# Turning x and h by VectorE blocks and a DRAM exchange instead of TensorE in a batched GRU and graph-convolution kernel

## The chip, the cores and the metric

The kernel runs on one core of a Trainium2 chip. The metric is the device time in microseconds of one execution of the whole program; lower is better. TensorE multiplies matrices into PSUM, VectorE and ScalarE do elementwise work, GpSimd (POOL) casts and issues DMAs, and SyncE (SP) only issues DMAs. Each engine works through its own queue in order.

## The reference

There are 16 graphs ("batches") of N = 1024 nodes with C = 128 features in fp32, each with a 1024 x 1024 adjacency matrix of zeros and ones. Two stages follow each other:

```python
h = relu(layernorm(x))
for i in range(4):                       # GRU stage
    hw = h @ weight[i]
    m = adj^T @ hw                       # einsum("bjn,bjd->bnd")
    gx, gh = m @ w_ih[i].T + b_ih[i], h @ w_hh[i].T + b_hh[i]
    r, z = sigmoid(xr + hr), sigmoid(xz + hz)
    n = tanh(xn + r * hn)
    h = (1 - z) * n + z * h
x = x + h * mask

h = relu(layernorm(x))
for i in range(4):                       # convolution stage
    h = relu(adj @ (h @ W[i]) + b[i])
    h = gamma * (h - mean) / sqrt(var + eps) + beta    # mean and var over all batches and nodes
x = x + h
```

Layer norm and the residual sum work on one node's 128 features, so they want nodes on the partitions. The gates' products contract over features, so they want features on the partitions. Between the two layouts an array of 1024 x 128 has to be turned, once on the way in (relu of the norm of x, to h_in) and once on the way out (the last h, to be added to x).

## The kernel before

**Streams.** The GRU stage keeps two batches in flight, in two `Stream` objects: `sa` has the even batches, `sb` the odd ones. `half_step(one, two)` (L856) interleaves them: it splits stream one's h for the aggregation (`split_step`), runs the gates of stream two (`gate_step`, L781), aggregates for stream one (`agg_step`), and in between calls the pieces that look ahead. Eight half-steps take two batches through four layers, so there are eight such cycles, and the last has no next batches.

**One half-step on TensorE.** The gates are 12 products (six for each half of 512 nodes), each of two passes (L790). `split_step` turns h into nodes on the partitions (hw_g, L498, 8 transposes), and ScalarE and VectorE split it into a high part (fp32r) and a low remainder, both named ghw (L502, L503). At layer 0 there is no such turn, since the norm's output y already has nodes on the partitions. `agg_step` then makes 32 products of 128 x 128 by 128 x 512 into two banks, pm (L525): eight row blocks, high and low, two halves. ScalarE copies pm to m (L770), which the next gates of that stream read.

**The gates' elementwise part.** ScalarE: sigmoid to r (L802), tanh (L807), sigmoid to z (L808). VectorE: L803, L804, then h minus r, times z, plus r (L810 to L812).

**Looking ahead.** When the stream that gates is past its layer i, `ahead` runs: after layer 0 (i = 1) `load_x` issues the load of x of batch b + 2 on POOL; after layer 1 (i = 2) `prepare` computes its norm: VectorE's statistics (L609, L610), ScalarE's root (L613), VectorE's reciprocal and shift (L616, L621), and eight ScalarE blocks y_in (L625); after layer 2 (i = 3) `prepare_turn` turns y_in by TensorE (pt_in, L647) into h_in (ScalarE copy, L648).

**The adjacency.** `look_on` acts for the stream that aggregates. At its layer 1 it issues eight raw copies on POOL (`copy_rows`, DRAM to DRAM, adj of batch b + 2 into raw), then for each of the batch's eight rows a POOL cast to bf16 (L594) and a DMA transpose on SP (L595), and last, on POOL, the write of the turned adjacency adjT_d (L848). At other layers VectorE looks over the rows (L589), reducing the low 16 bits of every entry to a maximum that a flag is made from at the end. `load_rows` (L581, in `take`) brings the next batch's rows from raw, eight loads of 512 KB on SP. A row tile comes free after the last layer's aggregation has read it.

**A batch's end.** After layer 3 `finish` runs `tail_norm`: TensorE turns the last h (pt_x, L657, two halves of four transposes), VectorE multiplies by the mask and adds to x (L660), statistics follow, and POOL writes xmid_d (L673). One half-step later the function `rest` does the remaining norm to y_mid (root, reciprocal, eight ScalarE blocks) and POOL writes ymid_d (L677). xmid_d and ymid_d feed the second stage.

**What sets the order.** Past a hand-ordered start, the queues of POOL and SP are in the order of the program text (`manual_schedule`). The order on TensorE, VectorE and ScalarE is set when the program is built, by a scheduler that may pull instructions forward or back; `behind` ties a piece to come after a given instruction. On POOL one cycle's order is: xmid of the even batch, ymid of the even batch, xmid of the odd, ymid of the odd, both x loads, eight raw copies, eight casts and adjT_d for the even batch, the same for the odd batch.

**The second stage** aggregates with the turned adjacency, loaded as bf16 from adjT_d by SP: `load_adjT` puts odd batches into one large block tile and even batches into half tiles (packed), then casts to fp32r (L1026, L1028).

Of the kernel before, what the change touches and what calls it, by code (L numbers as in the profile page):

```python
# [8 lines left out]
F32 = mybir.dt.float32  # L9
# [5 lines left out]
ALU = mybir.AluOpType  # L15
AX = mybir.AxisListType
P = 128
# [324 lines left out]
def exact_path(  # L342
# [191 lines left out]
    with ExitStack() as st:  # L534
# [42 lines left out]
        def load_rows(b):  # L577
# [4 lines left out]
                ts.append(t)  # L582
            return ts

        def look(b, row, j, part=0):

            lows = row.bitcast(U16).rearrange("p (n t) -> p n t", t=2)[:, :, 0]
            k = (b + part * B) * NB + j
            nc.vector.tensor_reduce(low[:, k : k + 1], lows, axis=AX.X, op=ALU.max)  # L589
# [46 lines left out]
            norm_scale(nt, 0, NB)  # L636
            norm_blocks(xt, y, nt, range(NB))

        def turn(y, name, hT=None, func=AF.Copy):

            if hT is None:
                hT = work.tile([P, N], F32, tag="h", name=f"h_{name}", bufs=7)
            for hf in range(NH):
                pt = tmp(f"pt_{name}_{hf}")
                for q in range(BH):
                    k = hf * BH + q
                    nc.tensor.transpose(pt[:, q * P : (q + 1) * P], y[:, k * P : (k + 1) * P], ident)  # L647
                nc.scalar.activation(hT[:, hf * HALF : (hf + 1) * HALF], pt, func)  # L648
            return hT

        def tail_norm(b, xt, hT):

            for hf in range(NH):
                pt = tmp(f"pt_x{b}_{hf}")
                for q in range(BH):
                    k = hf * BH + q
                    nc.tensor.transpose(pt[:, q * P : (q + 1) * P], hT[:, k * P : (k + 1) * P], ident)  # L657
                for q in range(BH):
                    k = hf * BH + q
                    nc.vector.scalar_tensor_tensor(  # L660
                        xt[:, k, :],
                        pt[:, q * P : (q + 1) * P],
                        maskT[:, b * NB + k : b * NB + k + 1],
                        xt[:, k, :],
                        ALU.mult,
                        ALU.add,
                    )
            nt = norm_stats(xt, f"mid{b}")
            if b + 1 < B:
# [3 lines left out]
            nc.gpsimd.dma_start(xmid_d[b].rearrange("(k p) c -> p k c", p=P), xt)  # L673

            def rest():
                norm_apply(xt, y, nt)
                nc.gpsimd.dma_start(ymid_d[b], y)  # L677

            return rest
# [10 lines left out]
        class Stream:  # L690


            def __init__(self, first):
                self.b, self.i, self.rest, self.tag = first, 0, None, "AB"[first % 2]
                self.opened = None

            def open(self, xt):

# [28 lines left out]
            def prepare(self, b, xt):  # L727
                y = work.tile([P, N], F32, tag=f"y{self.tag}", name=f"y_in{b}", bufs=1)
                norm(xt, y, f"in{b}")
                self.ready = b, xt, y  # L730

            def prepare_turn(self):
                b, xt, y = self.ready
                self.ready = xt, y, turn(y, f"in{b}")

            def take(self):
                self.xt, self.y, self.hT = self.ready
                self.rows = load_rows(self.b)
                self.looks = 0

            def split_step(self):
                nm = f"{self.b}_{self.i}"
# [38 lines left out]
            def gate_step(self, hf, between=None):  # L781
                i, nm = self.i, f"{self.b}_{self.i}_{hf}"
                if hf == 0 and not self.opened:
                    self.new = work.tile([P, N], F32, tag="h", name=f"h{nm}", bufs=7)
                cols = slice(hf * HALF, (hf + 1) * HALF)
                hin, m = self.hT[:, cols], self.m[hf]
                pr, pz, phn, pxn = self.opened or (acc(t, f"{t}{nm}") for t in ("g_r", "g_z", "g_hn", "g_xn"))

                def part(po, wT, g, rhs, start, stop):
                    nc.tensor.matmul(po, wT[:, i, g * C : (g + 1) * C], rhs, start=start, stop=stop)  # L790
# [12 lines left out]
                nc.vector.scalar_tensor_tensor(r, phn, b_hn(i), r, ALU.add, ALU.mult)  # L803
                nc.vector.tensor_add(r, pxn, r)  # L804
                if between:
                    between()
                nc.scalar.activation(r, r, AF.Tanh, bias=b_in(i))  # L807
                self.last_act = nc.scalar.activation(z, pz, AF.Sigmoid, bias=brz[:, 3 * i + 1 : 3 * i + 2])  # L808
                ho = self.new[:, cols]
                nc.vector.tensor_sub(ho, hin, r)  # L810
                nc.vector.tensor_mul(ho, ho, z)
                self.last_dve = nc.vector.tensor_add(ho, ho, r)  # L812
                if hf == NH - 1:
                    self.hT = self.new
                    self.i += 1

            def ahead(self):

                if self.b + 2 >= B:
                    return  # L820
                if self.i == 1:
                    self.next_x = load_x(self.b + 2, nc.gpsimd)
                if self.i == 2:
                    with behind(self.last_act, self.last_dve):
                        self.prepare(self.b + 2, self.next_x)
                if self.i == 3:
                    self.prepare_turn()

            def finish(self):

                if self.i == L:
                    assert self.looks == NB
                    self.rest = tail_norm(self.b, self.xt, self.hT)
                    self.b, self.i = self.b + 2, 0
                    if self.b < B:
                        self.take()

            def look_on(self, two):

                if self.i == 0:  # L840
                    return
                if self.i == 1:
                    if self.b + 2 < B:
                        copy_rows(self.b + 2)
                    adjT = turned_tile(f"adjT{self.b}")
                    for j in range(NB):
                        transpose_rows(self.b, self.rows[j], j, adjT)
                    nc.gpsimd.dma_start(adjT_d[self.b], adjT)  # L848
                if two.i == 2 and two.b + 2 < B:
                    return  # L850
                with behind(two.last_dve):
                    for j in range(self.looks, min(self.looks + 4, NB)):
                        look(self.b, self.rows[j], j)
                        self.looks += 1

        def half_step(one, two, gated=None, halfway=None):  # L856
# [9 lines left out]
            one.agg_step(0)  # L866
            if halfway:
                halfway()
            if one.rest:
                with behind(two.last_act):  # L870
                    one.rest()
                one.rest = None
            two.ahead()
            one.look_on(two)
            one.agg_step(1)
# [119 lines left out]
        with tc.manual_schedule(engines={mybir.EngineType.Pool, mybir.EngineType.SP}):  # L995
# [4 lines left out]
            sb.gate_step(0)  # L1000
            sb.gate_step(1)
            with tc.issue_after(sb.last_act.ins):
                sa.rest()
            sb.finish()


# [134 lines left out]
    def fetch_x(b):  # L1141
# [6 lines left out]
                t = t.rearrange("p l c -> p (l c)")  # L1148
                hs.extend(t[:, k * HALF : (k + 1) * HALF] for k in range(3))
        elif b == B - 1:  # L1150
            hs = [half_tile(f"xo_h{k}").bitcast(F32) for k in range(8)]
            row = keep.tile([P, N], F32, tag="row", name="xo_row", bufs=12)
            wide = turned_tile("xo_wide").rearrange("p a n -> p (a n)").bitcast(F32)
            hs.extend(t[:, k * HALF : (k + 1) * HALF] for t, n in ((row, 2), (wide, 8)) for k in range(n))
        else:
            return
        xo.extend(hs[k : k + 2] for k in range(0, len(hs), 2))
# [10 lines left out]
    for b in range(B):  # L1168
# [4 lines left out]
        if waiting:  # L1173
            last = first_weights(*waiting, stats)
            if b == 1:
                with tc.issue_after(last.ins):
                    sb.rest()
        if b == B - 1:
            hw_next = raw_split(1)
        aggregate(pm, hw, rows, 1)  # L1180
# [115 lines left out]
```

## Time and profile before

| what | value |
|---|---|
| median of 3 runs | 1840.78 us (1840.69 to 1840.88) |
| the profiled execution's own time | 1840.61 us |
| its span, first to last instruction | 1838.8 us |
| GRU stage / convolution stage, about | 1210 us / 628 us |
| mean granted TensorE clock | 0.999 |
| TensorE busy in 308 to 458 us / in 1210 to 1838 us | 150.00 of 150.00 us / 616.50 of 628.00 us |
| VectorE, ScalarE, POOL busy in 308 to 458 us | 100.77, 75.00, 31.48 us |
| mean share of the DMA engines busy in 308 to 458 us | 0.60 |
| pt_in and pt_x transposes | 128 and 128, 272 ns each (median) |

The span is 1.8 us shorter than the profiled execution's time; what is added or taken within the span comes in full in the time. A timeline line has the start in us, the busy time in us, the engine, the line, the operation, the tiles written and read, the shape and a count; in brackets stands how long the engine was idle before it and what ended that. Transposes in a row are pipelined, so eight of them that last 272 ns each take 1.03 us together, and the time from one group's start to the next group's start is what a group costs TensorE. L525 and L790 are the lines of helpers that record every aggregation product and every gate product, so one reads them by the tile's name.

### The profile page before, as it was taken

How to read it: one execution, taken by the hardware profiler on the slowest of the kernel's cores; microseconds unless marked ns; L12 is line 12 of the kernel's file. 1: busy time of each engine (PE TensorE's matmuls, PEld its weight loads, DVE VectorE, ACT ScalarE, POOL GpSimd, SP SyncE). 2: the span in 40 equal slices, each digit the busy share in tenths (PEclk: the TensorE clock that was granted, in tenths of full speed). 3: DMA queues.
4: the chain of work that ended last, by engine and by line, in shares of the span. 5: the costliest groups of instructions: out<-in, count | busy, mean ns of one | idle time of the engine just before them, and what ended most of it. 6: DMA issues, size and time to landing. Idle time of an engine off the chain costs nothing.

```text
span 1838.8 us, 21960 instructions
## 1 busy us (share of the span) xinstructions
PE 1821.5 (99%) x7326; PEld 1254.2 (68%) x7326; DVE 1225.6 (67%) x2244; ACT 1035.8 (56%) x1577; POOL 285.0 (15%) x378
## 2 busy tenths in 40 slices
PE   9999999999999999999999999999999999999997
PEld 6566666656566666666565666667778888888886
DVE  7656667567666766766766757676666666666665
ACT  5544454553545554445355353467777767767764
POOL 4131320230231042023023013011100000000011
PEclk9999999999999999999999999999999999999999
DMA  7189775575486386567557546349876676767676
GB/s 264 39 247 317 209 229 195 162 206 192 159 233 180 126 233 178 196 172 217 218 159 206 178 145 172 103 159 332 291 248 228 212 256 204 257 209 260 210 249 242
DMA packets 256280, 381.21 MB, mean 207 GB/s; under 512 B 149932, under 2 KB 155856, under 8 KB 252320
## 3 DMA queue, kind: packets, MB, share of 16 engines
q1 hardware_dynamic: 237968, 245.95, 44.2%
q0 software_dynamic: 17664, 133.53, 20.4%
q8 instruction: 59, 0.97, 0.2%
q14 instruction: 61, 0.50, 0.1%
q10 hardware_dynamic: 528, 0.26, 0.0%
HBM read 287.39 MB, written 117.44 MB: 220 GB/s over the span
## 4 chain that ended last, share of the span: by engine, by line
PE 94%; DVE 2%; ACT 2%; issue 1%; DMA 1%; SPq 0%; POOL 0%; DVEq 0%; ACTq 0%; POOLq 0%
PE pm L525 24%; PE pc_m L525 12%; PE g_r L790 11%; PE g_z L790 11%; PE pc_g_r L525 6%; PE pc_g_z L525 6%; PE g_hn L790 6%; PE g_xn L790 6%; PE hw_c L500 4%; PE hw_g L498 2%; PE pw_g_hn L1096 1%; PE pw_g_xn L1096 1%; PE pt_in L647 1%; PE pt_x L657 1%; PE pc_g_r L510 1%
## 5 line engine op out<-in xcount | busy, mean ns | idle before, releaser
L525 PE MATMUL pm<-row,ghw 128*128 128x512 f32 x2048 | 515.6, 406 | 0.1
L525 PEld LDWEIGHTS pm<-row,ghw 128*128 128x128 f32 x2048 | 383.2, 188 | 112.6 <-issue 36.9
L525 PE MATMUL pc_m<-wide,chw 128*128 128x512 f32 x1024 | 246.0, 395 | 0.0
L525 PEld LDWEIGHTS pc_m<-wide,chw 128*128 128x128 f32 x1024 | 190.5, 188 | 42.3 <-issue 4.3
L807 ACT ACTIVATE r<-r,vecs 128x512 f32<-128x512 f32 x128 | 92.3, 721 | 216.8 <-DVE r L804 216.8
L525 PE MATMUL pc_g_r<-wide,chw 128*128 128x512 f32 x464 | 187.0, 403 | 0.3 <-ACT chw L502 0.3
L525 PE MATMUL pc_g_z<-wide,chw 128*128 128x512 f32 x464 | 180.9, 390 | 0.0
L594 POOL CAST half<-row 128x1024 bf16<-128x1024 f32 x128 | 139.7, 1108 | 250.9 <-DMA adjT<-half 169.6
L1028 DVE CAST wide<-packed 128x1024 fp32r<-128x1024 bf16 x160 | 110.0, 692 | 74.5 <-PE pc_m L525 56.4
L1028 DVE CAST wide<-block 128x1024 fp32r<-128x1024 bf16 x160 | 110.2, 691 | 73.2 <-PE pc_g_z L525 40.2
L503 DVE TENSOR_TENSOR ghw<-hw_g,ghw 128x512 fp32r<-128x512 f32 x96 | 62.0, 686 | 129.7 <-ACT ghw L502 129.5
L1026 ACT CAST wide<-block 128x1024 fp32r<-128x1024 bf16 x96 | 100.6, 1048 | 59.3 <-PE pc_m L525 34.3
L803 DVE SCALAR_TENSOR_TENSOR r<-g_hn,vecs,r 128x512 f32<-128x512 f32 x128 | 95.4, 745 | 56.8 <-ACT r L802 31.3
L1026 ACT CAST wide<-packed 128x1024 fp32r<-128x1024 bf16 x96 | 100.7, 1049 | 55.6 <-PE pc_g_z L525 23.7
L790 PE MATMUL g_r<-m,w_mT 128*128 128x512 f32 x256 | 130.7, 592 | 0.0
L790 PE MATMUL g_z<-m,w_mT 128*128 128x512 f32 x256 | 130.7, 592 | 0.0
L790 PE MATMUL g_xn<-m,w_mT 128*128 128x512 f32 x256 | 130.7, 592 | 0.0
L589 DVE TENSOR_REDUCE low<-row 128x1 f32<-128x1024 uint16 x112 | 128.6, 1210 | 0.0
L808 ACT ACTIVATE z<-g_z,brz 128x512 f32<-128x512 f32 x128 | 87.1, 680 | 71.0 <-PE g_z L790 71.0
L770 ACT COPY m<-pm 128x512 f32<-128x512 f32 x128 | 68.8, 586 | 101.3 <-PE pm L525 101.2
L802 ACT ACTIVATE r<-g_r,brz 128x512 f32<-128x512 f32 x128 | 87.7, 685 | 60.3 <-PE g_r L790 59.5
L810 DVE TENSOR_TENSOR h<-h,r 128x512 f32<-128x512 f32 x96 | 74.6, 777 | 62.4 <-ACT r L807 62.4
(176 smaller groups left out, 2764.0 us busy)
## 6 DMA issues: line engine op xcount, KB each, us to landing
packed<-adjT_d SPq DMA_DIRECT2D x256, 256.0 KB, 5.9
block<-adjT_d SPq DMA_DIRECT2D x256, 256.0 KB, 5.4
raw<-in_adj_dram POOLq DMA_DIRECT2D x112, 512.0 KB, 11.6
row<-raw SPq DMA_DIRECT2D x112, 512.0 KB, 5.8
adjT_d<-adjT POOLq DMA_DIRECT2D x16, 2048.0 KB, 7.9
xmid_d<-x POOLq DMA_DIRECT2D x16, 512.0 KB, 4.8
y<-ymid_d POOLq DMA_DIRECT2D x16, 512.0 KB, 5.1
ymid_d<-y_mid POOLq DMA_DIRECT2D x15, 512.0 KB, 3.0
```

The lines of the kernel that those rows point to most:

```text
L500: nc.tensor.matmul(pt[:, q * P : (q + 1) * P], src, w, start=True, stop=True)
L525: nc.tensor.matmul(pm[hf], hw[s][:, j * P : (j + 1) * P], rows[j][:, hf * HALF : (hf + 1) * HALF], start=(j == 0 and s == 0), stop=(j == N ...
L589: nc.vector.tensor_reduce(low[:, k : k + 1], lows, axis=AX.X, op=ALU.max)
L594: nc.gpsimd.tensor_copy(t, row.bitcast(F32))
L790: nc.tensor.matmul(po, wT[:, i, g * C : (g + 1) * C], rhs, start=start, stop=stop)
L802: nc.scalar.activation(r, pr, AF.Sigmoid, bias=brz[:, 3 * i : 3 * i + 1])
L803: nc.vector.scalar_tensor_tensor(r, phn, b_hn(i), r, ALU.add, ALU.mult)
L807: nc.scalar.activation(r, r, AF.Tanh, bias=b_in(i))
L808: self.last_act = nc.scalar.activation(z, pz, AF.Sigmoid, bias=brz[:, 3 * i + 1 : 3 * i + 2])
L810: nc.vector.tensor_sub(ho, hin, r)
L1026: nc.scalar.copy(r, t)
L1028: nc.vector.tensor_copy(r, t)
```

## The change

For batches 2 to 15 on the way in and 0 to 13 on the way out, the turn is no longer made by TensorE. VectorE's transpose turns 32 x 32 blocks, each in its place among the partitions. `blocks_out` makes two such calls of 128 x 512 for an array, into half tiles, and SP writes each to a DRAM tile `cross` (256 KB); `exchange_in` reads it back with four DMAs of 32 partitions each, in which every partition takes four runs of 128 elements from four others. The features of a group of nodes then lie in an order that `by_nodes` and `four_ways` describe: the gate products of layer 0 read h_in through `by_nodes` (runs of 32 elements) and write PSUM through `four_ways`, and the sums of `tail_norm` read the exchanged tile with the same pattern from SBUF, where they read PSUM before. Batches 0 and 1 in and 14 and 15 out keep the TensorE turn; so do the turns between layers (hw_g).

With it, times of issue change. `finish` now starts both exchanges (of the coming batch's y_in and of the old batch's h) and leaves what follows in a list `ends`: `arrive`, with the reads from DRAM; then `tail_norm` with the sums and statistics; then its rest. Each later half-step takes one from the list (`end_step`). `load_x` moves from i = 1 to i = 2 and `prepare` from i = 2 to i = 3, `prepare_turn` is gone, and the looks pause at i = 3 instead of i = 2. As a result one cycle's order on POOL is: xmid even, ymid even, xmid odd, eight raw copies, eight casts and adjT_d of the even batch, ymid odd, x load for the even stream, eight raw copies, eight casts and adjT_d of the odd batch, x load for the odd stream. On SP the exchange's writes and reads stand among the DMA transposes and the row loads. In the second stage `load_adjT` and the tiles of the last loads of x swap the parts of even and odd batches.

```diff
--- before.py
+++ after.py
@@ -582,6 +582,17 @@
                 ts.append(t)
             return ts
 
+        def exchange_out(t, name):
+            d = rawd.tile([P, HALF], F32, tag="cross", name=f"cross_{name}", bufs=8)
+            nc.sync.dma_start(d, t)
+            return d
+
+        def exchange_in(d, t):
+
+            src = d.rearrange("(t r) (s x) -> s r t x", t=4, s=4)
+            for s in range(4):
+                nc.sync.dma_start(t[s * 32 : (s + 1) * 32, :].rearrange("r (t x) -> r t x", t=4), src[s])
+
         def look(b, row, j, part=0):
 
             lows = row.bitcast(U16).rearrange("p (n t) -> p n t", t=2)[:, :, 0]
@@ -636,10 +647,8 @@
             norm_scale(nt, 0, NB)
             norm_blocks(xt, y, nt, range(NB))
 
-        def turn(y, name, hT=None, func=AF.Copy):
-
-            if hT is None:
-                hT = work.tile([P, N], F32, tag="h", name=f"h_{name}", bufs=7)
+        def turn(y, name, hT, func=AF.Copy):
+
             for hf in range(NH):
                 pt = tmp(f"pt_{name}_{hf}")
                 for q in range(BH):
@@ -648,23 +657,39 @@
                 nc.scalar.activation(hT[:, hf * HALF : (hf + 1) * HALF], pt, func)
             return hT
 
-        def tail_norm(b, xt, hT):
-
+
+
+        def by_nodes(cols):
+            return cols.rearrange("c (q k i) -> c k q i", q=4, i=32)
+
+        def four_ways(cols):
+            return cols.rearrange("p (k a c) -> p k a c", a=4, c=32)
+
+        def blocks_out(src, name):
+
+            ds = []
             for hf in range(NH):
-                pt = tmp(f"pt_x{b}_{hf}")
+                t = half_tile(f"t_{name}_{hf}").bitcast(F32)
+                last = nc.vector.transpose(by_nodes(t), four_ways(src[:, hf * HALF : (hf + 1) * HALF]))
+                ds.append(exchange_out(t, f"{name}_{hf}"))
+            return ds, last
+
+        def tail_norm(b, xt, hT, parts=None):
+
+            for hf in range(NH):
+                if parts:
+                    pt = by_nodes(parts[hf])
+                else:
+                    pt = tmp(f"pt_x{b}_{hf}")
+                    for q in range(BH):
+                        k = hf * BH + q
+                        nc.tensor.transpose(pt[:, q * P : (q + 1) * P], hT[:, k * P : (k + 1) * P], ident)
+                    pt = four_ways(pt)
                 for q in range(BH):
                     k = hf * BH + q
-                    nc.tensor.transpose(pt[:, q * P : (q + 1) * P], hT[:, k * P : (k + 1) * P], ident)
-                for q in range(BH):
-                    k = hf * BH + q
-                    nc.vector.scalar_tensor_tensor(
-                        xt[:, k, :],
-                        pt[:, q * P : (q + 1) * P],
-                        maskT[:, b * NB + k : b * NB + k + 1],
-                        xt[:, k, :],
-                        ALU.mult,
-                        ALU.add,
-                    )
+                    xk = xt[:, k, :].rearrange("p (a c) -> p a c", a=4)
+                    mask = maskT[:, b * NB + k : b * NB + k + 1]
+                    nc.vector.scalar_tensor_tensor(xk, pt[:, q, :, :], mask, xk, ALU.mult, ALU.add)
             nt = norm_stats(xt, f"mid{b}")
             if b + 1 < B:
                 y = work.tile([P, N], F32, tag="h", name=f"y_mid{b}", bufs=7)
@@ -691,8 +716,8 @@
 
 
             def __init__(self, first):
-                self.b, self.i, self.rest, self.tag = first, 0, None, "AB"[first % 2]
-                self.opened = None
+                self.b, self.i, self.tag = first, 0, "AB"[first % 2]
+                self.opened, self.across, self.ends = None, False, []
 
             def open(self, xt):
 
@@ -727,16 +752,14 @@
             def prepare(self, b, xt):
                 y = work.tile([P, N], F32, tag=f"y{self.tag}", name=f"y_in{b}", bufs=1)
                 norm(xt, y, f"in{b}")
-                self.ready = b, xt, y
-
-            def prepare_turn(self):
-                b, xt, y = self.ready
-                self.ready = xt, y, turn(y, f"in{b}")
+                self.ready = xt, y
 
             def take(self):
-                self.xt, self.y, self.hT = self.ready
+                self.xt, self.y = self.ready
                 self.rows = load_rows(self.b)
-                self.looks = 0
+                self.looks, self.across = 0, True
+                self.hT = work.tile([P, N], F32, tag="h", name=f"h_in{self.b}", bufs=7)
+                return blocks_out(self.y, f"in{self.b}")[0]
 
             def split_step(self):
                 nm = f"{self.b}_{self.i}"
@@ -784,9 +807,14 @@
                     self.new = work.tile([P, N], F32, tag="h", name=f"h{nm}", bufs=7)
                 cols = slice(hf * HALF, (hf + 1) * HALF)
                 hin, m = self.hT[:, cols], self.m[hf]
+                across = self.across and i == 0
+                if across:
+                    hin = by_nodes(hin)
                 pr, pz, phn, pxn = self.opened or (acc(t, f"{t}{nm}") for t in ("g_r", "g_z", "g_hn", "g_xn"))
 
                 def part(po, wT, g, rhs, start, stop):
+                    if rhs is hin and across:
+                        po = four_ways(po)
                     nc.tensor.matmul(po, wT[:, i, g * C : (g + 1) * C], rhs, start=start, stop=stop)
 
                 part(pr, w_hhT, 0, hin, True, False)
@@ -807,7 +835,10 @@
                 nc.scalar.activation(r, r, AF.Tanh, bias=b_in(i))
                 self.last_act = nc.scalar.activation(z, pz, AF.Sigmoid, bias=brz[:, 3 * i + 1 : 3 * i + 2])
                 ho = self.new[:, cols]
-                nc.vector.tensor_sub(ho, hin, r)
+                if across:
+                    nc.vector.tensor_sub(four_ways(ho), hin, four_ways(r))
+                else:
+                    nc.vector.tensor_sub(ho, hin, r)
                 nc.vector.tensor_mul(ho, ho, z)
                 self.last_dve = nc.vector.tensor_add(ho, ho, r)
                 if hf == NH - 1:
@@ -818,22 +849,40 @@
 
                 if self.b + 2 >= B:
                     return
-                if self.i == 1:
+                if self.i == 2:
                     self.next_x = load_x(self.b + 2, nc.gpsimd)
-                if self.i == 2:
+                if self.i == 3:
                     with behind(self.last_act, self.last_dve):
                         self.prepare(self.b + 2, self.next_x)
-                if self.i == 3:
-                    self.prepare_turn()
 
             def finish(self):
 
-                if self.i == L:
-                    assert self.looks == NB
-                    self.rest = tail_norm(self.b, self.xt, self.hT)
-                    self.b, self.i = self.b + 2, 0
-                    if self.b < B:
-                        self.take()
+                if self.i < L:
+                    return
+                assert self.looks == NB
+                args = self.b, self.xt, self.hT
+                self.b, self.i = self.b + 2, 0
+                ins = self.take() if self.b < B else None
+                if not ins:
+                    self.ends = [tail_norm(*args)]
+                    return
+                h_in = self.hT
+                outs, last = blocks_out(args[-1], f"out{args[0]}")
+                parts = [half_tile(f"n_{args[0]}_{hf}").bitcast(F32) for hf in range(NH)]
+
+                def arrive():
+                    for hf in range(NH):
+                        exchange_in(ins[hf], h_in[:, hf * HALF : (hf + 1) * HALF])
+                    for hf in range(NH):
+                        exchange_in(outs[hf], parts[hf])
+                    self.ends.append(lambda: self.ends.append(tail_norm(*args, parts)))
+
+                self.ends = [arrive]
+
+            def end_step(self, *after):
+                if self.ends:
+                    with behind(*after):
+                        self.ends.pop(0)()
 
             def look_on(self, two):
 
@@ -846,7 +895,7 @@
                     for j in range(NB):
                         transpose_rows(self.b, self.rows[j], j, adjT)
                     nc.gpsimd.dma_start(adjT_d[self.b], adjT)
-                if two.i == 2 and two.b + 2 < B:
+                if two.i == 3 and two.b + 2 < B:
                     return
                 with behind(two.last_dve):
                     for j in range(self.looks, min(self.looks + 4, NB)):
@@ -866,10 +915,8 @@
             one.agg_step(0)
             if halfway:
                 halfway()
-            if one.rest:
-                with behind(two.last_act):
-                    one.rest()
-                one.rest = None
+            one.end_step(two.last_act)
+            two.end_step(two.last_dve)
             two.ahead()
             one.look_on(two)
             one.agg_step(1)
@@ -1000,7 +1047,7 @@
             sb.gate_step(0)
             sb.gate_step(1)
             with tc.issue_after(sb.last_act.ins):
-                sa.rest()
+                sa.ends.pop()()
             sb.finish()
 
 
@@ -1017,9 +1064,9 @@
 
     def load_adjT(b, i):
         ts = []
-        block = turned_tile(f"block{b}_{i}") if b % 2 else None
+        block = None if b % 2 else turned_tile(f"block{b}_{i}")
         for j in range(NB):
-            t = block[:, j, :] if b % 2 else half_tile(f"packed{b}_{i}_{j}")
+            t = half_tile(f"packed{b}_{i}_{j}") if b % 2 else block[:, j, :]
             nc.sync.dma_start(t, adjT_d[b][:, j, :])
             r = row_tile(f"wide{b}_{i}_{j}")
             if j % 3 == 1:
...
```

More of the change, by code (lines that the diff above doesn't have):

```diff
@@ L1150, in fetch_x @@
         elif b == B - 1:
-            hs = [half_tile(f"xo_h{k}").bitcast(F32) for k in range(8)]
+            wide = turned_tile("xo_wide").rearrange("p a n -> p (a n)").bitcast(F32)
             row = keep.tile([P, N], F32, tag="row", name="xo_row", bufs=12)
-            wide = turned_tile("xo_wide").rearrange("p a n -> p (a n)").bitcast(F32)
-            hs.extend(t[:, k * HALF : (k + 1) * HALF] for t, n in ((row, 2), (wide, 8)) for k in range(n))
+            hs = [t[:, k * HALF : (k + 1) * HALF] for t, n in ((wide, 8), (row, 2)) for k in range(n)]
+            hs.extend(half_tile(f"xo_h{k}").bitcast(F32) for k in range(8))
         else:
@@ L1176, in exact_path @@
                 with tc.issue_after(last.ins):
-                    sb.rest()
+                    sb.ends.pop()()
         if b == B - 1:
```

## The prediction

> **What bounds the kernel now.** I read the page's busy shares and its chain first.
>
> ```profile
> PE 1821.5 (99%) x7326; PEld 1254.2 (68%) x7326; DVE 1225.6 (67%) x2244; ACT 1035.8 (56%) x1577; POOL 285.0 (15%) x378
> ...
> PE 94%; DVE 2%; ACT 2%; issue 1%; DMA 1%; SPq 0%; POOL 0%; DVEq 0%; ACTq 0%; POOLq 0%
> ```
>
> TensorE sets the end and hardly ever waits: each TensorE instruction removed is worth its start-to-start time, and every new wait of TensorE is paid in full. TensorE's timeline prices a turn:
>
> ```profile
> 281.48 4.22 PE L525 MATMUL pm<-row,ghw 128*128 128x512 f32 x16
> 285.54 1.03 PE L647 MATMUL pt_in<-ident,y_in 128*128 128x128 f32 x8
> 286.33 3.89 PE L525 MATMUL pm<-row,ghw 128*128 128x512 f32 x16
> 290.06 1.03 PE L498 MATMUL hw_g<-ident,h 128*128 128x128 f32 x8
> ...
> 300.83 7.85 PE L525 MATMUL pm<-row,ghw 128*128 128x512 f32 x32
> 308.52 1.03 PE L657 MATMUL pt_x<-ident,h 128*128 128x128 f32 x8
> 309.39 1.02 PE L790 MATMUL g_r<-h,w_hhT 128*128 128x512 f32 x2
> ```
>
> The 32 products with a turn inside take 290.06 - 281.48 = 8.58 us, without it 308.52 - 300.83 = 7.69: a pt_in costs 0.89, a pt_x 309.39 - 308.52 = 0.87.
>
> A cycle is eight half-steps for an even and an odd batch. I count from zero at C, the half-step whose gates are the new even batch's layer 0 (477.58 in the cycle shown); D has the odd batch's layer-0 gates, A the even batch's layer 3, B the odd one's. From B to B it takes 149.7. The order that the change moves is POOL's, in its timeline:
>
> ```profile
> 475.99 0.54 POOL L677 DMA_DIRECT2D ymid_d<-y_mid  x1 [13.30 <-ACT y_mid L625]
> 481.54 0.92 POOL L673 DMA_DIRECT2D xmid_d<-x  x1 [5.01 <-DVE mv_mid L610]
> 494.46 0.54 POOL L677 DMA_DIRECT2D ymid_d<-y_mid  x1 [12.00 <-ACT y_mid L625]
> 495.01 1.80 POOL L540 DMA_DIRECT2D x<-in_x_dram  x2
> 496.80 2.95 POOL L575 DMA_DIRECT2D raw<-in_adj_dram  x6
> ...
> 531.81 0.56 POOL L848 DMA_DIRECT2D adjT_d<-adjT  x1 [3.62 <-DMA adjT<-half]
> 532.36 3.37 POOL L575 DMA_DIRECT2D raw<-in_adj_dram  x7
> ...
> 568.99 0.55 POOL L848 DMA_DIRECT2D adjT_d<-adjT  x1 [3.59 <-DMA adjT<-half]
> ```
>
> Both x loads go out at +17.4, before any adjacency work. The work from the first raw copy to the second adjT_d then fills 496.80 to 568.99 = 72.2 (70.6 to 72.9 in other cycles).
>
> [...] when eight row loads, an adjT_d and an xmid_d meet (window 165 to 180), they land after
>
> ```profile
> row<-raw SPq DMA_DIRECT2D x8, 512.0 KB, 12.7
> adjT_d<-adjT POOLq DMA_DIRECT2D x1, 2048.0 KB, 12.5
> xmid_d<-x POOLq DMA_DIRECT2D x1, 512.0 KB, 14.5
> ```
>
> where the page's medians are 5.8, 7.9 and 4.8. [...]
>
> **Removed.** Turns into batches 2 to 15 and out of 0 to 13: 14 x 0.89 + 14 x 0.87 = -24.6 us, or -3.5 in each of 7 cycles. ACT's 28 copies of h_in go too; ACT isn't the bound.
>
> **Added.** 56 VectorE transposes of 128x512. [...] I take 0.7, near the plain 128x512 operation (0.69): 39 us on an engine busy 67%, hidden behind TensorE's 18.45 us half-steps; at 2.4 it would be 134 us and show, some +20. 56 writes and 224 exchange reads on SP at 0.32 us of issue: the even batch's reads land about five us into B for C, the odd one's five us into C for D, 10 or more us of margin, so 0; the row loads behind them start some six us later, the same margin, 0. Their 29 MB are 8% more traffic. The 84 layer-0 gate products of h_in read runs of 32 elements; a product with such a moving operand isn't in the trace. At full rate 0; at half rate two passes of 0.43 each twice, 84 x 0.86 = +72. The weight loads of strided operands cost 211 ns against 140, but skip elements, which these runs don't: I take 0. Second stage: packed and block swap parities, symmetric: 0 (up to 3 if batch 0's block waits for the last adjT_d).
>
> **Moved.** This decides. tail_norm comes half to one half-step later, load_x moves from i = 1 to i = 2 and prepare from 2 to 3. On POOL each x load thus falls behind all of its batch's raw copies, casts and adjT_d, and the even raw copies behind the odd xmid. Step by step, for the odd batch:
> - In D the built order puts 19 of the 32 aggregation products (7 to 14 in the first cycles) ahead of the odd gates, which end at about +34. The even y_mid follows them on ACT: z to about +35.5, table load 1.3, root and copies about 1, eight blocks of 0.4: ymid at +41, xmid at +41.5, raw copies from +42.4 (before +19.2).
> - 71.6 us of unchanged adjacency work, plus a ymid (0.55) and an even x (0.9): second adjT_d at +115.5, odd x issued at +116.6 (before +17.4).
> - SP's row loads for the next even batch follow the last DMA transpose at +114, so eight of them, adjT_d and x burst together as in the window above: x lands 14.5 later, at +131.1 (at the earliest +124, if adjT_d alone slows it).
> - Then the norm, priced by VectorE and ScalarE in the cycle shown:
>
> ```profile
> 528.66 0.47 DVE L609 BATCH_NORM_STATS2 st_in<-x 128x6 f32<-128x128 f32 x2
> ```
>
> ```profile
> 530.94 0.30 ACT L613 ACTIVATE rs_in<-mv_in,eps_t 128x8 f32<-128x8 f32 x1 [3.29 <-DVE mv_in L610]
> 531.71 3.19 ACT L625 ACTIVATE y_in<-x,ms_in,rs_in 128x128 f32<-128x128 f32 x8 [0.47 <-DVE ms_in L621]
> 534.80 1.04 ACT L770 COPY m<-pm 128x512 f32<-128x512 f32 x2
> ```
>
> Sums to root 2.6, and VectorE is in order, so the second half of A's gates (add, multiply, t_out, add, about 2.9 more) stands between the stats and the reciprocal; eight y_in 3.2; tanh 0.7, high split 0.6, copy of pm 0.6: the m that B's gates need is 10.7 after landing, at +141.8. Both engines' later work queues behind this x: hence TensorE stops.
> - TensorE wants that m at +131.5 (17.6 for C, six half-steps of 18.45 less turns, plus the waits below): it waits 141.8 - 131.5 = **10.3** a cycle. x in by +121 means no wait; +124 means about 3.
>
> Two smaller waits: C's m copy is queued behind the later tail (0.6), and E's g_r bank is held by a sigmoid behind y_mid's table load (1.2): 1.8 a cycle, 0.7 in the two with few products ahead. [...]
>
> **Sum.** Late odd x: batches 5 to 15, six cycles (batch 3's load stands early, the last cycle has none). Four late ones: -3.5 + 1.8 + 10.3 + 1.7 = +10.3 each, 41.2. Two early ones: with fewer products ahead D's gates and so x come 3 earlier, TensorE 1.1 earlier, the norm's chain is 0.4 longer, so the wait is 10.3 - 3 + 1.1 + 0.4 = 8.8; -3.5 + 0.7 + 8.8 + 1.7 = +7.7 each, 15.4. First -3.5, last +1.8. Together +54.9: 1840.6 + 54.9 = **1895.5 us**, said as 1895. The runs' median, 1840.78, is 0.2 above the profiled time; that changes nothing. A change of 0.2% (3.7 us) is about what the measurement can tell from none.
>
> **Rivals.** (1) *x is late, but less*: the exchange moved the row loads, so the burst may miss x. Landing at +125 gives 4 us of wait a cycle without the clock's part, six cycles, the small waits staying (4 x 1.8 + 2 x 0.7 + 1.8 = 10.4): -24.6 + 10.4 + 24 = +9.8; 1845 to 1860. For it: 4.8 and 7.9 are the usual landings. Against: the last transpose releases SP just as POOL issues x. (2) *The other side, x in time*: if adjacency work, freed of the collision with x and tail, ran 10 us shorter, or TensorE were 10 us later for another reason, landing comes before +121, no wait, and the removed turns show: 1840.6 - 24.6 + 0 to 10 = 1816 to 1826. For it: casts waited up to 9.66 us in the shown cycle for row or transpose. Against: the spread over cycles is only 2.3 us. (3) *Costlier operations*: transposes at 2.4 us or half rate for h_in on top of the late x: 1915 to 1965. That the change doesn't do what it says is excluded by the built order: 224 turns are gone from TensorE, 56 transposes stand on VectorE.
>
> **How the numbers follow.** Main 0.53; less late 0.20; in time 0.15, all faster; costlier 0.09; near balance, within 0.2%, 0.03. Faster 0.15 plus 0.01 of less late = 0.16, same 0.03, slower 0.81. Range: 1848, inside the less-late case, to 1920, which takes in a costlier transpose; it leaves out the faster side and half rate. The likeliest alone: 1875 to 1910.
>
> **What would show it.** Right: POOL's timeline has each odd x load directly behind adjT_d, near +116, landing near +130; TensorE's waits sit before B's first product of m, ended by ACT's m, some 10 us in six cycles; pt_in and pt_x are down to 32 transposes of 256; cycles take about 160. Wrong: x landing by +121 or B starting without a wait; TensorE waiting in C or D for h_in (exchange late); layer-0 gate products above 0.43 us a pass[...].

## The result and the profile after

The changed kernel takes 1901.35 us (median; 1898.56 to 1904.04) against 1840.74 us for the kernel before: the ratio is 1.033, 95% interval 1.0312 to 1.0348. The change made the kernel slower by 61 us. The profiled execution took 1898.56 us, with a span of 1896.6 us, so it is 57.95 us longer than the profiled execution of before (1840.61 us).

The first part of the page of the kernel after, busy time and share of the span, and the row of granted TensorE clock over 40 slices:

```profile
PE 1815.0 (96%) x7102; PEld 1234.4 (65%) x7102; DVE 1252.2 (66%) x2300; ACT 1028.0 (54%) x1555; POOL 286.6 (15%) x378
...
PEclk9999998999999899899999989999999999999999
```

The 224 turns are gone (7326 to 7102 instructions on TensorE), yet TensorE is now idle for 4% of the span, and four slices of the clock row, all in the GRU stage, show an 8. The chain of waits, which carried the reading of before, breaks off in this page after its last instruction, so TensorE's list of waits takes its place (the total in us, how often, the longest):

```profile
PE g_r L818 <- ACT m L793: 55.1, 8, 12.2
PE g_r L818 <- ACT r L830: 7.1, 7, 3.8
...
PE g_xn L818 <- ACT m L793: 2.2, 5, 0.5
```

Before, TensorE had no listed wait for m at all, and for the sigmoid r only this one:

```profile
PE g_r L790 <- ACT r L802: 0.9, 1, 0.9
```

Nearly all of the new wait is in six places, 3.45, 11.58, 10.61, 9.53, 6.86 and 12.20 us, each ahead of the first product of m in the odd batch's layer-3 gates. TensorE's timeline at the third of them (start, busy time, then what is computed; in brackets the idle time and what ended it):

```profile
622.95 1.02 PE L818 MATMUL g_r<-h,w_hhT 128*128 128x512 f32 x2
634.58 2.08 PE L818 MATMUL g_r<-m,w_mT 128*128 128x512 f32 x2 [10.61 <-ACT m L793]
636.45 1.91 PE L818 MATMUL g_hn<-h,w_hhT 128*128 128x512 f32 x2
638.15 1.09 PE L818 MATMUL g_xn<-m,w_mT 128*128 128x512 f32 x2
639.08 1.02 PE L818 MATMUL g_z<-h,w_hhT 128*128 128x512 f32 x2
```

Here B's gates wait for 10.6 us, and the products behind the wait take 1.87 and 1.70 us from start to start where the others take 0.86. The granted clock is 0.50 from 628.1 to 638.2 us, and 1.00 in 615 to 628 and in 638.4 to 650. To see why m is late, follow POOL in the same cycle. Its C, where the count starts, is at 492.87:

```profile
533.65 0.56 POOL L702 DMA_DIRECT2D ymid_d<-y_mid  x1 [24.79 <-ACT y_mid L636]
535.88 0.91 POOL L698 DMA_DIRECT2D xmid_d<-x  x1 [1.66 <-DVE low L600]
536.77 3.44 POOL L575 DMA_DIRECT2D raw<-in_adj_dram  x7
...
609.27 0.56 POOL L897 DMA_DIRECT2D adjT_d<-adjT  x1 [3.74 <-DMA adjT<-half]
609.82 0.93 POOL L540 DMA_DIRECT2D x<-in_x_dram  x1
```

The odd x goes out at 609.82, that is at +116.9. It meets the row loads; the DMA issues of 609 to 630 us (count, size each, median us from issue to landing):

```profile
row<-raw SPq DMA_DIRECT2D x4, 512.0 KB, 16.0
adjT_d<-adjT POOLq DMA_DIRECT2D x1, 2048.0 KB, 12.4
x<-in_x_dram POOLq DMA_DIRECT2D x1, 512.0 KB, 14.9
cross_in<-t_in SPq DMA_DIRECT2D x2, 256.0 KB, 16.8
```

VectorE waits for the landing with everything queued behind it:

```profile
624.73 0.49 DVE L620 BATCH_NORM_STATS2 st_in<-x 128x6 f32<-128x128 f32 x2 [12.60 <-DMA x<-in_x_dram]
```

and ScalarE makes the eight blocks of y_in before it copies pm to m:

```profile
627.55 0.30 ACT L624 ACTIVATE rs_in<-mv_in,eps_t 128x8 f32<-128x8 f32 x1 [13.07 <-DVE mv_in L621]
...
629.75 3.17 ACT L636 ACTIVATE y_in<-x,ms_in,rs_in 128x128 f32<-128x128 f32 x8
632.83 0.71 ACT L835 ACTIVATE r<-r,vecs 128x512 f32<-128x512 f32 x1
633.44 0.61 ACT L776 CAST ghw<-y_in 128x512 fp32r<-128x512 f32 x1
633.95 1.06 ACT L793 COPY m<-pm 128x512 f32<-128x512 f32 x2
```

The copy of pm has nothing to do with x: pm was full at about 623. It is late only because ScalarE works in order.

### The profile page after: what moved, and what is told of

It is laid out like the page before. It is cut to its first block, busy times and chain, and to the rows that moved or that the text cites. A ratio compares the mean times of both kernels' runs of the same rounds, so it can differ in the third digit from the quotient of the medians.

```text
span 1896.6 us, 22006 instructions
## 1 busy us (share of the span) xinstructions
PE 1815.0 (96%) x7102; PEld 1234.4 (65%) x7102; DVE 1252.2 (66%) x2300; ACT 1028.0 (54%) x1555; POOL 286.6 (15%) x378
## 5 line engine op out<-in xcount | busy, mean ns | idle before, releaser
L525 PEld LDWEIGHTS pm<-row,ghw 128*128 128x128 f32 x2048 | 383.4, 188 | 116.9 <-issue 38.3
L818 PE MATMUL g_r<-m,w_mT 128*128 128x512 f32 x256 | 137.4, 619 | 55.1 <-ACT m L793 55.1
L818 PEld LDWEIGHTS g_r<-m,w_mT 128*128 128x128 f32 x256 | 48.9, 195 | 120.1 <-ACT m L793 73.1
```

What stands on the lines that cost most here:

```text
L525: nc.tensor.matmul(pm[hf], hw[s][:, j * P : (j + 1) * P], rows[j][:, hf * HALF : (hf + 1) * HALF], start=(j == 0 and s == 0), stop=(j == N ...
```

## The experiments

The theory: the loss is the odd x, which lands late for two reasons together, its place on POOL behind the adjacency work and the later tail ahead of that work. The rivals: the exchange itself costs the time (traffic, issues, VectorE's transposes), or x behind the adjacency work is enough. 

**The layer shift alone, on the kernel before.**

```diff
-                if self.i == 1:
+                if self.i == 2:
                     self.next_x = load_x(self.b + 2, nc.gpsimd)
-                if self.i == 2:
+                if self.i == 3:
                     with behind(self.last_act, self.last_dve):
                         self.prepare(self.b + 2, self.next_x)
-                if self.i == 3:
-                    self.prepare_turn()
...
+                        self.prepare_turn()
                         self.take()
...
-                if two.i == 2 and two.b + 2 < B:
+                if two.i == 3 and two.b + 2 < B:
```

> The kernel before with the layer shift alone: load_x at i = 2 (behind the raw copies, casts and adjT_d of its batch), prepare at i = 3, the TensorE turn of y_in at the batch's end; no exchange, tail_norm and its rest where they were. Theory (two moves are needed together, the x behind the adjacency work and the later tail ahead of it): raw copies still start near +19, the odd x goes out near +92 and lands by +107, before the +121 from which it decides: no wait, 1838 to 1846. Rival (x behind the adjacency work is enough): six waits of about 10 us, 1890 to 1915.

Measured: 1843.60 us, ratio 1.0013, interval 1.0006 to 1.0019. In POOL's timeline of this kernel (C at 479.44) x stands behind adjT_d as in the changed kernel, but the raw copies begin at +18.3:

```profile
497.16 0.56 POOL L677 DMA_DIRECT2D ymid_d<-y_mid  x1 [12.85 <-ACT y_mid L625]
497.71 3.89 POOL L575 DMA_DIRECT2D raw<-in_adj_dram  x8
...
571.50 0.56 POOL L847 DMA_DIRECT2D adjT_d<-adjT  x1 [3.71 <-DMA adjT<-half]
572.05 0.93 POOL L540 DMA_DIRECT2D x<-in_x_dram  x1
```

The odd x goes out at +92.6, where +92 was expected, and lands 9.1 us later, at +101.7. No wait over 0.4 us for m appears; seven such waits add up to 2.9 us, about the 2.2 us of the result. So x behind the adjacency work isn't enough. In the changed kernel x goes out 24 us later still, because the raw copies begin at +43.9 there, behind the later tail. No run has the later tail without the exchange.

**Both x loads one layer earlier, on the changed kernel** (`self.i == 2` back to `self.i == 1` at the load alone).

> The changed kernel with one edit: both x loads go out one layer earlier (i = 1), so on POOL's queue they stand ahead of the raw copies and casts. Theory (the loss is the odd x that lands late, by way of the norm, y_in and the copy of pm): TensorE's waits of 3 to 12 us ahead of layer 3's odd gates are gone, and with them the slow products behind them; the removed turns show: 1840.7 - 24.6 + 6 to 10 for the small waits = 1822 to 1828, faster than before. Rival (the exchange itself costs the time, by its DMA traffic, SP issues or VectorE's transposes): the waits stay in other places and the time stays above 1845.

Measured: 1853.14 us, ratio 1.007, interval 1.0053 to 1.0087. 48 us of the loss are gone, and the waits for m with them, as the theory said. But its number, 1822 to 1828, missed by 25 us, and the rival's came in: waits in other places, and a time above 1845. Taken alone, this run can't reject the rival. TensorE's list of waits names a new one:

```profile
PE g_r L818 <- DMA h_in<-cross_in: 10.7, 11, 2.8
PE pm L525 <- DMA row<-raw: 4.0, 9, 1.0
PE g_r L818 <- ACT m L793: 3.3, 8, 0.5
```

Now the exchange is late. It is the largest new wait, but not the whole loss: against the kernel before, TensorE is idle for 18.4 us more, and its aggregation products take 8.4 us more from start to start (510.2 against 501.8 us, idle time left out). POOL's timeline of one cycle:

```profile
363.04 0.90 POOL L540 DMA_DIRECT2D x<-in_x_dram  x1 [23.87 <-ACT y_mid L636]
363.93 0.56 POOL L702 DMA_DIRECT2D ymid_d<-y_mid  x1
364.49 0.90 POOL L698 DMA_DIRECT2D xmid_d<-x  x1
380.91 0.89 POOL L540 DMA_DIRECT2D x<-in_x_dram  x1 [15.53 <-DVE low L600]
381.79 3.43 POOL L575 DMA_DIRECT2D raw<-in_adj_dram  x7
```

The four tiles of x are all in use: a new x can only go into the tile that y_mid of the batch two back is still made from. (The second wait's label names one of VectorE's looks, which ends at about the same time; the eight y_mid on ScalarE end at 380.61, and x goes out at 380.91.) Placed that early, the odd x holds POOL for 15.5 us, and the raw copies behind it start at +58.7 instead of +43.9. The adjacency work, the row loads behind it on SP and the t_in write behind those move with it, and h_in comes up to 2.8 us after C wants it. The expectation had forgotten the tile.

**Each VectorE transpose made twice, on top of that.**

```diff
-                last = nc.vector.transpose(by_nodes(t), four_ways(src[:, hf * HALF : (hf + 1) * HALF]))
+                for _ in range(2):
+                    last = nc.vector.transpose(by_nodes(t), four_ways(src[:, hf * HALF : (hf + 1) * HALF]))
```

> As the first experiment (x loads early), and each VectorE transpose of the exchange made twice (56 more of 0.70 us). Theory (VectorE's transposes are hidden): within 4 us of the first experiment. Rival (they are on the path): 39 us more.

Measured: 1851.66 us (1849.63 to 1855.00), 1.5 us below the 1853.14 it is to be compared with, and inside that one's own 1848.56 to 1856.65: 39 us more on VectorE cost nothing that shows. The transposes are hidden.

**Only the odd x moved, by one place:** between the last cast and the adjT_d of its batch.

```diff
-                if self.i == 2:
+                if self.i == 2 and (self.tag == "A" or written[0]):
                     self.next_x = load_x(self.b + 2, nc.gpsimd)
...
+                    if self.tag == "B" and self.b + 2 < B:
+                        self.next_x = load_x(self.b + 2, nc.gpsimd)
                     nc.gpsimd.dma_start(adjT_d[self.b], adjT)
```

> The changed kernel with the odd x load moved up by one place on POOL: between the last cast and the adjT_d of its batch, some 4.5 us sooner; the even x and all else as changed. Theory (the wait follows the landing one to one, threshold near +121): issued near +112.5, landing with the row loads' burst near +126: waits of about 6 instead of 10.6 us in five or six cycles, 1868 to 1880; if without adjT_d ahead of it it lands in 8 us, no wait and 1822 to 1832. Rival (something else, the row loads or the exchange, sets the wait): waits and time unchanged, 1895 to 1905.

Measured: 1896.05 us, ratio 1.0295, interval 1.0276 to 1.0313. The number is the rival's, by a road that neither had named. The edit changed the built order too: 7 instead of 19 aggregation products stand ahead of the odd gates, and on ScalarE the eight y_in now stand ahead of the copies of pm for A's gates (the even batch's layer 3), one half-step sooner than before B's. In one cycle (C at 331.10) x is issued at +109.9 and lands at +115.4, which is ahead of the +121 from which B would have been safe; but now A needs it. ScalarE, VectorE's first statistics, which mark the landing, and TensorE's product that waited:

```profile
449.58 3.18 ACT L636 ACTIVATE y_in<-x,ms_in,rs_in 128x128 f32<-128x128 f32 x8
452.67 1.04 ACT L793 COPY m<-pm 128x512 f32<-128x512 f32 x2
```

```profile
446.52 0.48 DVE L620 BATCH_NORM_STATS2 st_in<-x 128x6 f32<-128x128 f32 x2 [8.61 <-DMA x<-in_x_dram]
```

```profile
453.28 2.08 PE L818 MATMUL g_r<-m,w_mT 128*128 128x512 f32 x2 [7.77 <-ACT m L793]
```

The product comes 6.76 us after the landing, at +122.2, and was wanted at +114.4. In the five other cycles the distance is 6.77 each; in the changed kernel it is 9.84 or 9.85 in four cycles, and 10.70 and 11.63 in the first two. So the wait is still the landing's, but the deadline isn't +121 for good: it is where the built order of ScalarE and VectorE puts the norm, and this order moved it some 14 us forward, to about 114.4 - 6.8 = +107.6, while x moved only some 16 us.

**Both x loads side by side,** at the even stream's i = 2: ahead of the odd batch's raw copies, and after the tile is free.

```diff
-                if self.i == 2:
-                    self.next_x = load_x(self.b + 2, nc.gpsimd)
+                if self.i == 2 and self is sa:
+                    for st in (sa, sb):
+                        st.next_x = load_x(st.b + 2, nc.gpsimd)
```

> The changed kernel, with the odd x load moved beside the even one (both at the even stream's i = 2): ahead of the odd batch's raw copies, casts and adjT_d, and late enough that its tile is free, unlike in the first experiment, where POOL stood 15 us for it. Theory: no wait for m ahead of layer 3's odd gates. The second adjT_d comes near +127 and the even t_in write still lands behind eight row loads, so h_in may be up to 2 us late at C: 1826 to 1845. Rival (the odd x is not what sets the 10 us wait): 1890 to 1905. Second rival (the exchange is late by its traffic, wherever the x stand): as in the first experiment, 1848 to 1857.

Measured: 1827.59 us (1826.20 to 1828.71), ratio 0.9929, interval 0.9913 to 0.9946: faster than the kernel before by 13 us. The order of TensorE, VectorE and ScalarE is the same, instruction for instruction, as in the run with the odd x moved by one place (1896.05 us); so is SP's order, and POOL's but for the odd x. The place of the odd x on POOL alone is worth 1896.05 - 1827.59 = 68.5 us. So the gain over the changed kernel isn't the built order's, which these two runs share. The run with both loads one layer earlier (1853.14 us) has this order on the three engines too, and POOL's order but for the x loads; SP's differs only early on, for the first batches. So the 25.5 us between these two hang on where the x loads stand, and this rejects the rival that the exchange itself costs them. POOL's timeline (C at 470.11):

```profile
546.59 0.54 POOL L702 DMA_DIRECT2D ymid_d<-y_mid  x1
547.12 1.81 POOL L540 DMA_DIRECT2D x<-in_x_dram  x2
548.92 2.00 POOL L575 DMA_DIRECT2D raw<-in_adj_dram  x4
...
588.52 0.56 POOL L898 DMA_DIRECT2D adjT_d<-adjT  x1 [4.03 <-DMA adjT<-half]
```

Both x have landed by 559.31, that is by +89.2, well ahead of +107.6. TensorE's waits for m shrink from 55.1 to

```profile
PE g_r L818 <- ACT m L793: 4.1, 10, 0.7
```

No wait for h_in and none for a row's load from raw is listed. The exchange, its 29 MB and its 280 issues are all there, so they are not the loss.

**The same with the t_in writes ahead of the row loads on SP:**

```diff
-                self.rows = load_rows(self.b)
...
-                return blocks_out(self.y, f"in{self.b}")[0]
+                ins = blocks_out(self.y, f"in{self.b}")[0]
+                self.rows = load_rows(self.b)
+                return ins
```

> As the run with both x loads side by side, and on SP the two t_in writes go ahead of the eight row loads instead of behind them. Theory (h_in is late in C because its write waits behind the row loads' burst; the 10 us wait of the changed kernel covered this): t_in lands in some 3 us instead of 16, h_in is there before C, no wait for it; the removed turns show: 1820 to 1832, faster than the kernel before. Rival (the reads of h_in themselves are slowed by the row loads and adjT_d): waits of 1 to 3 us stay in C, 1835 to 1850.

Measured: 1827.23 us (1825.21 to 1828.17), ratio 0.9923, interval 0.9906 to 0.9939. Within the theory's numbers, but no different from the run above. The t_in writes do land sooner: after 2.4 us (median), against 11.4 us in the run above, where they stand behind the row loads. The reads of h_in, now beside the row loads, take up to 10.8 us, against at most 2.8 in the run above; but TensorE has no listed wait for them. In the run above the write behind the rows was in time already (h_in's reads start at 605.9 and C comes at 618.4), so this run doesn't test what made h_in late with the early loads. That the place of the x loads made it late is shown by the pair above; the steps between are read from the trace only.

**Idle transposes into the wait,** on the changed kernel:

```diff
+            if two is sb and two.i == 3 and 3 < two.b < B and not written[0]:
+                pt = tmp(f"pt_fill{two.b}")
+                for k in range(80):
+                    nc.tensor.transpose(pt[:, k % 4 * P : (k % 4 + 1) * P], ident, ident)
             two.gate_step(0)
```

> The changed kernel with 80 transposes of the identity (about 8.7 us of TensorE, their result unused) ahead of layer 3's gates of batches 5 to 13, where TensorE waits about 10 us for m. Theory (a second cost hangs on the idle: after it three products of two passes take 4.5 us instead of 2.6 because the clock was lowered): the wait shrinks to some 2 us, the products behind it run at 0.86 us again, the granted clock rises from 0.98 to above 0.99, and the time falls by up to 1.9 x 5 = 10 us, 1884 to 1900. Rival (the products are slow for another reason): they stay slow, and the time is 1898 or more.

Measured: 1894.64 us (1892.73 to 1897.60), against 1898.56 to 1904.04 without: 400 instructions more, and 6.7 us less. The granted clock is 0.995 where it was 0.982. The wait in the first affected cycle has no fill and stays as it was. TensorE's timeline behind one fill:

```profile
780.85 8.89 PE L912 MATMUL pt_fill<-ident 128*128 128x128 f32 x80
789.58 1.02 PE L818 MATMUL g_r<-h,w_hhT 128*128 128x512 f32 x2
790.44 1.02 PE L818 MATMUL g_r<-m,w_mT 128*128 128x512 f32 x2
791.30 1.02 PE L818 MATMUL g_hn<-h,w_hhT 128*128 128x512 f32 x2
```

The products behind it run at 0.86 us at once. Behind three others of the five fills, after waits of 0.89 to 1.64 us, the first pair takes 0.96 us and the next 0.86. Behind the first, a wait of 2.27 us was left, and the products behind that took up to 1.71 us. So the slow products are a matter of the idle time before them. The built order differs here as well (again 7 products), so the 6.7 us need not be the clock's alone; the verdict rests on the pace of the products.

## Why the prediction was right

It said 1895 us and the measured time is 1901, for the mechanism that it gave. Against the profiled execution the sum reads (products and turns are priced from start to start, idle time left out):

| term | predicted | in the trace |
|---|---|---|
| turns removed | -24.6 | pt_in 12.6 to 1.7, pt_x 13.8 to 1.6: -23.1 |
| waits of B behind the late x | 4 x 10.3 + 2 x 8.8 = +58.8 | the six listed for m, 54.2, and 3.8 for the sigmoid in the first of these cycles: +58.1 |
| small waits | +10.4 | (2.2 + 55.1 - 54.2) + (7.1 - 3.8 - 0.9) = +5.5 |
| lowered clock behind the waits | 6 x 1.7 = +10.2 | products over 0.86 us behind seven waits: +14.5 |
| not in the sum | | +3.0 (aggregation products +3.8, the rest -0.8) |
| sum | +54.8 | +57.95 |

The large term is right. That the total comes within 3 us is in part luck: the errors of the smaller terms cancel. The small waits were put 5 us too high and the turns 1.5 us, the clock was put 4 us too low, and 3 us were not thought of.

**The moves on POOL.** In the cycle shown: y_mid's write at +40.8 (said +41), raw copies +43.9 (+42.4), second adjT_d +116.4 (+115.5), x issued +116.9 (+116.6), landed +131.9 (+131.1), B wanting m at +131.1 (+131.5) and getting it at +141.7 (+141.8). The chain from landing to m was 9.85, a little shorter than the 10.7 worked out, and the landing a little later. From C to C this cycle takes 160.4 us (said about 160). Over the cycles the wait isn't even: 3.45 to 12.20 us, where 8.8 and 10.3 were said, and the errors cancel in the total. The smallest is in the first affected cycle, ahead of which 3.84 us had gone to the wait for a sigmoid that stood behind the same late norm.

**The clock.** A mis-sized term: the 1.7 us for each wait was the author's estimate, and the trace of before shows no lowered clock (mean 0.999). The trace of after shows 1.2 to 3.0 us, 2.1 on average, behind each of seven waits over 3 us (the seventh is the one for the sigmoid), 14.5 in all, at a granted clock of 0.50. Each slowed one to four of the two-pass products, by up to 1.2 us.

**The added operations.** A VectorE transpose of 128x512 took 0.71 us (into t_in) and 0.67 (into t_out). The 0.7 that was said was the author's estimate, near the plain 128x512 operation (0.69). The transposes are hidden, as the doubled run shows on top of the early loads. Layer 0's products of h_in in runs of 32 run at 0.86 us for two passes, as products of h do: the +72 us bound falls to 0. The sums that read the exchanged tile take 0.35 us (median), those from PSUM 0.34.

**The margin of the exchange** was said to be 10 us or more. It is less: with the x loads side by side the even reads are issued over 605.9 to 609.5 and C comes at 618.4, so with 2.0 us of landing 7 us are left; the odd reads have landed by 633.9 and D comes at 639.6, 5.7 us later. The experiment with the early loads used these up. In the changed kernel the wait in B stood ahead of C and covered this.

**The rivals.** "In time" was priced at 1816 to 1826 and given 0.15. The run with the x loads side by side comes out at 1827.6, 1.6 us above that range. Its profiled span is 14.5 us below that of before, and TensorE's starts account for this: turns -23.2, idle time +5.2 (of which 4.1 for m, where before had none), gate products +2.4, aggregation products +1.1. So the rival's price was nearly right, and what separated it from the forecast was the landing of x. "Costlier operations" has nothing for it. Both moves were needed, as the sum had it: the shift alone costs 2 us, the exchange with the x in time gains 13, and both with the x behind the adjacency work lose 61.

## What to carry to other kernels

When work is moved past other work on an in-order queue, price when it is issued and when it lands, against the moment that someone needs it; what it costs is the difference, and the queue's own busy share (15% here) says nothing of it. Look also, in the built order, at what is queued behind the instruction that waits: the copy of pm, ready 11 us before, was held by a norm of a batch that was not due yet. An instruction that moves to a better place can fail for another reason there, its buffer: the same load cost 68 us in one place, held its queue for 15 us in another, and was free in a third.

## What the runs showed of the hardware that was not expected

TensorE's products were slow after idles shorter than the smallest of the six waits in B (3.45 us) too. In the experiment with the early loads it idled for 2.75 us, and its next two pairs took 1.84 and 1.60 us from start to start, where the changed kernel shows 1.70 to 1.87 at a granted clock of 0.50:

```profile
475.58 2.04 PE L818 MATMUL g_r<-h_in,w_hhT 128*128 128x512 f32 x2 [2.75 <-DMA h_in<-cross_in]
477.42 1.77 PE L818 MATMUL g_r<-m,w_mT 128*128 128x512 f32 x2
479.02 1.02 PE L818 MATMUL g_hn<-h_in,w_hhT 128*128 128x512 f32 x2
```

With the fills the same followed an idle of 2.27 us (1.71 and 1.43 us behind the first pair's 1.23). After idles of 1.59 and 1.83 us in the kernel with the early loads the first pair shows a busy time of 1.10, near the usual 1.02, and the next pair runs at 0.86 again.

And the landing of the same DMA changed with what was issued just before it on its own queue: the t_in writes of 256 KB landed after 11.4 us (median) behind the row loads and after 2.4 us ahead of them, in two kernels that differ in this order alone. In the changed kernel two of them took 16.8 us (median) behind eight row loads and beside an adjT_d and an x, and a t_out write of the same size 2.0 us where little else was under way (the DMA engines' mean busy share is 0.09 from 628.1 to 638.2 us).
